# Feed-forward weights fetched from inside the plan and turned by the vector engine; variance of the last row pair by accumulated sums

## The chip, the cores and the metric

The kernel runs on one NeuronCore of a Trainium2 chip. The metric is the time of one execution on the device in microseconds (us), the median of several runs. A core has five engines that work side by side, each with its own queue of instructions taken strictly in order: PE (matrix products; its weight loads are shown apart as PEld), DVE (vector work), ACT (activation functions), POOL (general vector work) and SP, which here only issues DMA transfers. An instruction that waits holds up all that stands behind it on its engine.

## The reference

One transformer block on `x` of 4096 rows by 256 columns, all in float32: attention in which a row sees itself and the 127 rows before it, then a feed-forward part that mixes each row with the one before, a layer norm after each.

```python
q = (x @ Wq + bq)            # 16 heads of 16, 4 groups; k and v: 4 heads of 16
scores = q k^T / 4, masked to  i-128 < j <= i
x = layernorm(x + softmax(scores) v @ Wo + bo)
x_prev = x shifted down by one row
r = sigmoid((mu_r*x + (1-mu_r)*x_prev) @ W_r.T)
k = (mu_k*x + (1-mu_k)*x_prev) @ W_k.T
out = layernorm(x + r * (square(relu(k)) @ W_v.T))
```

`layernorm` subtracts the row's mean and divides by the root of its variance plus 1e-5. The three feed-forward weights are needed turned (columns on partitions), as `x` is for its products.

## The kernel before

The 4096 rows are cut into 8 chunks of 512 (index `c`) and 16 pairs of two 128-row blocks (index `p`, blocks `b`). The work of a chunk or pair is written as small operations, `op(kind, ...)`, each for one engine, with what it reads and writes, the ring buffers and PSUM banks that it takes, and a rank. `Plan.run` (L267) then fixes, at build time, the order of every engine's queue: the table `KINDS` (L34) gives each kind its engine, an assumed length and a rank; on PE the order is written out by hand in `ORDER` (L112), step by step; on the other engines, SP's queue included, the operation that can start first goes first, and among those within `WAIT` of it the one of lowest rank. Nothing is reordered on the chip.

A PE "step" below is one operation of `ORDER`. The kinds, with the line of their matmuls:

- `q` (L778, two per chunk) and `kv` (L730): projections from the turned `x` (`xT`); ACT copies them out of PSUM (`q copy` L789, `kv copy` L739). `vT` (L753) turns the v part; DVE copies it (L758).
- `q move` (L800): four DMAs on SP that copy half of the chunk's `q` to other partitions. The next kind needs all four.
- `maxima`, `maxima 2` (L842/L833 for masks, L855 for scores): row maxima of the scores of a pair, three steps for a pair, each on four of the eight PSUM banks; DVE reduces them (L865, two instructions a step, each frees two banks), turns the result (`nm turn`, L875), and four DMAs put it beside `q` (`nm put`, L879).
- `weights a` (two per pair) and `weights b` (L942 with masks L914/L928): scores again, now transposed, with the maxima taken off; ACT takes exponentials (L979, L1013). They need `nm put`.
- `values` (L1040, L1053), `wo` (L1180): the attention's output and projection; DVE turns and scales between them; then the norm (`plan_norm` L1107: statistics on DVE, scale on POOL, apply on ACT L1136).
- `fk` (L1296), `fr` and `fv` (L1323): the feed-forward products; between them ACT takes relu (L1306) and tanh (L1337), POOL the square (L1310) and the sum (L1355), DVE the gate (L1350).

Loads at the start stand in SP's queue in the order of the program text (L467 to L527): `x` of pairs 0 and 1, `Wk`, `Wv`, `Wq`, `x` of pairs 2 and 3, `W_k`, `W_r`, `W_v`, `Wo` (four DMAs), `bo`, `mu_r`, `mu_k`; after them come the planned ones. To the plan these are `given`, with an assumed time of landing, and `begin ...` stands for what each engine has to do before its first planned operation.

`x` is turned in one of two ways. For chunks 0 and 1 (pairs 0 to 3) PE transposes it against an identity, in four matmuls a pair (L619, and steps `xT`, L698), and ACT (or DVE) copies it out of PSUM. From chunk 2 on (`p > 3`, L683) a pair is loaded in four DMAs whose pieces are 256-byte runs (`turned_rows`, L452), so placed that one DVE instruction, which transposes 32 by 32 squares, finishes it (`turn_squares`, L458). The feed-forward weights are turned on PE (steps `w`, L666: four matmuls each) and copied out by ACT with a factor (L674; 0.5 for `W_v`).

The last pair (p = 15) has an own ending, `plan_last` (L1376), for each of its two blocks: PE product (L1383), gate (DVE L1395), sum (DVE L1399), statistics (DVE L1402, L1403), epsilon (DVE L1404), root (POOL L1409), apply (DVE L1414), store (L1419; the first from SP's queue, the second from ACT's).

Of the kernel before, what the change touches and what calls it, by code (L numbers as in the profile page):

```python
# [34 lines left out]
    "given": (SP, 0.0, -553.88),  # L35
    "begin pe": (PE, 1.7, 0),
    "begin act": (ACT, 6.5, -483.57),
    "begin dve": (DVE, 8.5, -417.58),
    "begin pool": (POOL, 5.3, -536.56),
    "begin sp": (SP, 8.0, -360.66),  # L40
    "w": (PE, 0.43, 0),
    "w copy": (ACT, 0.62, 0.22),
    "x load": (SP, 0.5, -0.16),
    "x turn": (DVE, 0.7, 28.13),
    "xT": (PE, 0.43, 0),
    "xT copy": (ACT, 0.6, -59.9),
    "kv": (PE, 1.72, 0),
    "kv copy": (ACT, 0.69, -12.4),
    "vT": (PE, 0.43, 0),
    "vT copy": (DVE, 0.4, -22.77),  # L50
    "ones": (SP, 0.6, -32.64),
    "q": (PE, 1.72, 0),
    "q copy": (ACT, 0.69, 43.86),
    "q move": (SP, 2, -8.69),
    "maxima": (PE, 0.88, 0),
    "maxima 2": (PE, 0.6, 0),
    "reduce": (DVE, 1.14, 17.06),
    "reduce 2": (DVE, 0.81, 10.47),
    "nm turn": (DVE, 0.21, -30.81),
    "nm put": (SP, 2.3, -10.21),  # L60
    "weights a": (PE, 0.95, 0),
    "exp a": (ACT, 1.02, 13.73),
    "weights b": (PE, 1.07, 0),
    "exp b": (ACT, 1.02, -18.72),
    "values": (PE, 2.7, 0),
    "oN": (DVE, 1.25, -54.27),
    "rs": (DVE, 0.35, 29.15),
    "at": (DVE, 0.9, 2.41),
    "attT": (DVE, 0.44, 30.81),
    "xres": (SP, 0.5, 55.18),  # L70
    "bo": (POOL, 1.3, -22.9),
    "wo": (PE, 1.72, 0),
    "y": (DVE, 0.69, 34.29),
    "x1T first": (POOL, 0.25, 45),
    "x1 out": (SP, 0.45, -21.17),
    "x1 in": (SP, 0.5, -30.3),
    "x1 turn": (DVE, 0.7, 32.58),
    "x1T": (PE, 0.43, 0),
    "x1T copy": (ACT, 0.6, -17.18),
    "xd": (POOL, 1.3, -31.81),  # L80
    "xm": (DVE, 0.45, 57.86),
    "fk": (PE, 1.72, 0),
    "relu": (ACT, 0.6, 20.57),
    "square": (POOL, 1.07, 41.45),
    "fr": (PE, 1.72, 0),
    "gate": (ACT, 0.6, 36.74),
    "fv last": (PE, 0.86, 0),
    "y2 last": (DVE, 0.42, -24.81),
    "stats last": (DVE, 1.1, 59.97),
    "scale last": (POOL, 0.8, -21.85),  # L90
    "apply last": (DVE, 0.46, -51.24),
    "fv": (PE, 1.72, 0),
    "y2": (DVE, 0.69, -26.87),
    "y2 add": (POOL, 1.3, 33.09),
    "y2 add late": (DVE, 0.69, 28.33),
    "store": (SP, 0.45, 32.89),
    "stats y": (DVE, 0.6, 21.13),
    "scale y": (POOL, 1.5, 51.83),
    "apply y": (ACT, 0.6, 31.11),
    "stats y2": (DVE, 0.6, 46.62),  # L100
    "scale y2": (POOL, 1.5, 26.69),
    "apply y2": (ACT, 0.6, 80.48),
# [4 lines left out]
    "x load": 0.45, "x1 in": 0.45, "q move": 1.6, "xres": 1.3, "x1 out": 1.3, "store": 1.3,  # L107
# [9 lines left out]
        5, 11, 19, 23, 37, 98, 105, 134,  # L117
    ],
    "q": [
        1, 2, 6, 13, 16, 26, 46, 51, 60, 76, 81, 92, 119, 124, 130, 138,  # L120
    ],
    "vT": [
        7, 36, 22, 66, 45, 115, 150, 173,
    ],
    "w": [
        29, 30, 10,
    ],
    "maxima": [
        9, 12, 17, 15, 32, 25, 35, 28, 48, 39, 62, 57, 73, 59, 75, 84,
        89, 100, 104, 91, 121, 118, 125, 110, 131, 145, 153, 137, 167, 156, 176, 171,  # L130
    ],
    "maxima 2": [
        8, 14, 24, 20, 47, 61, 56, 88, 99, 103, 117, 107, 144, 136, 152, 170,
    ],
    "weights a": [
        18, 27, 31, 38, 41, 44, 50, 52, 65, 68, 70, 77, 79, 86, 93, 95,
        112, 114, 123, 127, 133, 140, 147, 149, 158, 165, 174, 179, 185, 188, 192, 194,
    ],
    "weights b": [
        21, 34, 42, 53, 64, 71, 80, 96, 108, 128, 141, 159, 163, 180, 183, 189,  # L140
    ],
    "values": [
        33, 43, 49, 63, 72, 85, 90, 109, 122, 132, 146, 164, 175, 184, 193, 199,
    ],
    "wo": [
        40, 54, 69, 78, 83, 101, 111, 116, 142, 148, 160, 172, 182, 190, 198, 204,
    ],
    "fk": [
        55, 74, 87, 102, 120, 143, 151, 157, 162, 168, 186, 197, 201, 207, 209, 212,
    ],  # L150
    "fr": [
        58, 82, 97, 106, 126, 135, 155, 161, 169, 181, 191, 195, 203, 206, 211, 214,
    ],
    "fv": [
        67, 94, 113, 129, 139, 154, 166, 177, 178, 187, 196, 200, 205, 210, 213,
    ],
    "xT": [
        3, 4,
    ],
    "x1T": [  # L160
        202, 208,
    ],
    "fv last": [
        215, 216,
# [47 lines left out]
class Plan:  # L212
# [8 lines left out]
    WAIT = 0.35  # L221
# [145 lines left out]
def postln_block(  # L367
# [112 lines left out]
    def load_w(dst, w):  # L480
        nc.sync.dma_start(out=dst, in_=w.rearrange("(c p) n -> p c n", p=P))
        return dst

# [10 lines left out]
    for p in range(2, 4):  # L494
        load_x(p)
    ffn_l = {"r": wl_r, "k": wl_k, "v": wl_v}
    for k, w in (("k", W_k), ("r", W_r), ("v", W_v)):
        load_w(ffn_l[k], w)

    wo = const.tile([P, 2, D], F32, tag="wo", name="wo")  # L500
    for g in range(NG):
        nc.sync.dma_start(
            out=wo[32 * g : 32 * (g + 1), :, :],
            in_=Wo[64 * g : 64 * (g + 1), :].rearrange("(rp x) n -> x rp n", x=32),
        )
    bo_b = const.tile([P, D], F32, tag="bo_b", name="bo_b")
    nc.sync.dma_start(out=bo_b, in_=bo.partition_broadcast(P))


# [4 lines left out]
    muT = const.tile([P, 2, C2], F32, tag="muT", name="muT")  # L514
    with nc.allow_non_contiguous_dma(reason="small vectors, once"):
        for i, bias in enumerate((bk, bv)):
            nc.scalar.dma_start(
                out=rows[2:3, :].rearrange("o (g i d) -> o i g d", g=NG, i=2)[:, i],
                in_=bias.rearrange("(o g d) -> o g d", o=1, g=NG),
            )  # L520
        for o in range(2):
            nc.scalar.dma_start(
                out=rows[0:2, :].rearrange("r (g o d) -> o r g d", g=NG, o=2)[o],
                in_=bq.rearrange("(g o r d) -> o r g d", g=NG, o=2, d=DH)[o],
            )
        for w, mu in enumerate((mu_r, mu_k)):
            nc.sync.dma_start(out=muT[:, w, :], in_=mu.rearrange("(p c) -> p c", c=C2))  # L527
# [131 lines left out]
    def plan_weight(k, base, scale):  # L659
        key = ("wps", k)  # L660

        def turn():
            w4 = bank(key).rearrange("p (i o n) -> p i o n", i=C2, o=C2)
            for o in range(C2):
                for i in range(C2):
                    nc.tensor.transpose(  # L666
                        w4[:, i, o, :],
                        ffn_l[k][:, o, i * P : (i + 1) * P] if k == "v" else columns(ffn_l[k][:, o, :], i),
                        ident,
                    )  # L670

        def keep():
            ffnT[k] = const.tile([P, C2, D], F32, tag=f"w{k}T", name=f"w{k}T")
            nc.scalar.mul(ffnT[k], bank(key).rearrange("p (i n) -> p i n", i=C2), scale)  # L674

        op("w", base, turn, r=[("rest", k)], w=[("wps", k)], banks=[(key, 1)], mode="full")
        op("w copy", base, keep, r=[("wps", k)], w=[("w", k)], uses=[("wps", k)])
# [4 lines left out]
    def plan_load(p):  # L682
        if p > 3:  # L683
# [3 lines left out]
        else:  # L687
            op("given", p, lambda: None, w=[("x", p)], new=[(ring("x", 4), ("x", p))], late=(3.7, 4.5, 7.0, 7.8)[p])

    def plan_xT(p, base):  # L690
        c, h = divmod(p, 2)
        key = ("xT", c, h)

        def turn():
            ps = bank(key).rearrange("p (c b n) -> p c b n", c=C2, b=2)
            for ch in range(C2):
                for b in range(2):
                    nc.tensor.transpose(  # L698
# [815 lines left out]
```

## Time and profile before

| | |
|---|---|
| median of 3 runs | 346.14 us (344.85 to 346.62) |
| the profiled execution, its own time | 345.45 us |
| its span, first to last instruction | 343.7 us |
| PE busy | 331.5 us, 4729 matmuls |
| DVE busy | 268.9 us |
| ACT, POOL busy | 165.8, 124.8 us |
| mean granted PE clock | 0.986 |

The span is 1.75 us shorter than the time of the same execution; what lies around the span stays outside the profile. "Busy" of PE is modelled: matmuls overlap, so a stretch that shows PE as busy need not be free of waiting, and it is the starts of the matmuls that tell. The first 15 us carry the loads: the profile shows 242 GB/s there from 6.8 to 15.0 us against a mean of 72.

### The profile page before, as it was taken

How to read it: one execution, taken by the hardware profiler on the slowest of the kernel's cores; microseconds unless marked ns; L12 is line 12 of the kernel's file. 1: busy time of each engine (PE TensorE's matmuls, PEld its weight loads, DVE VectorE, ACT ScalarE, POOL GpSimd, SP SyncE). 2: the span in 40 equal slices, each digit the busy share in tenths (PEclk: the TensorE clock that was granted, in tenths of full speed). 3: DMA queues.
4: the chain of work that ended last, by engine and by line, in shares of the span. 5: the costliest groups of instructions: out<-in, count | busy, mean ns of one | idle time of the engine just before them, and what ended most of it. 6: DMA issues, size and time to landing. Idle time of an engine off the chain costs nothing.

```text
span 343.7 us, 11149 instructions
## 1 busy us (share of the span) xinstructions
PE 331.5 (96%) x4729; PEld 221.7 (64%) x4729; DVE 268.9 (78%) x494; ACT 165.8 (48%) x227; POOL 124.8 (36%) x220
## 2 busy tenths in 40 slices
PE   8899999999999999999999999999999999999991
PEld 6455566655765676567666656767767676678871
DVE  7067787778888859999789998698948897678675
ACT  2402554556337583272442645653762386834541
POOL 5200000111404334161326231427632765648773
PEclk9969999999999999999999999999999999999998
DMA  6842333121511243211123220322221224210002
GB/s 191 226 100 47 75 78 68 35 67 19 139 33 35 69 89 94 67 33 58 42 60 98 63 68 32 65 82 84 55 87 41 65 70 120 79 49 31 32 31 92
DMA packets 55062, 24.65 MB, mean 72 GB/s; under 512 B 40644, under 2 KB 54852, under 8 KB 55012
## 3 DMA queue, kind: packets, MB, share of 16 engines
q1 hardware_dynamic: 54832, 23.81, 26.3%
q8 instruction: 37, 0.61, 0.8%
q10 hardware_dynamic: 180, 0.13, 0.1%
q14 instruction: 13, 0.11, 0.1%
HBM read 13.64 MB, written 7.86 MB: 63 GB/s over the span
## 4 chain that ended last, share of the span: by engine, by line
PE 83%; DVE 7%; SPq 3%; POOL 2%; issue 1%; DMA 1%; ACT 1%; POOLq 0%; DVEq 0%
PE ps L1323 14%; PE ps L942 12%; PE ps L855 9%; PE ps L1040 8%; PE ps L1180 8%; PE ps L778 8%; PE ps L1296 7%; PE ps L1053 4%; PE ps L730 4%; PE ps L842 2%; PE ps L914 2%; DVE xm L1268 2%; SPq L800 2%; DVE nm L865 1%; PE ps L753 1%
## 5 line engine op out<-in xcount | busy, mean ns | idle before, releaser
L865 DVE TENSOR_REDUCE nm<-ps 128x6 f32<-128x960 f32 (+1 forms) x96 | 94.7, 1037 | 16.6 <-PE ps L855 15.0
L979 ACT ACTIVATE prA<-ps 128x1024 f32<-128x1024 f32 x64 | 63.2, 1024 | 56.7 <-PE ps L914 53.1
L942 PE MATMUL ps<-qT,kT 17*64 17x512 f32 (+1 forms) x1024 | 54.7, 499 | 0.0
L855 PE MATMUL ps<-kT,qT 16*128 16x160 f32 x1024 | 48.8, 309 | 2.4 <-DMA qT<-qT 2.3
L1124 POOL TENSOR_SCALAR ve_y<-mv_y 128x2 f32<-128x2 f32 x31 | 8.0, 257 | 96.2 <-DVE mv_y L1119 95.3
L855 PEld LDWEIGHTS ps<-kT,qT 16*128 16x128 f32 x1024 | 39.5, 188 | 4.6 <-DMA qT<-qT 3.3
L1268 DVE SCALAR_TENSOR_TENSOR xm<-xd,muT,x1T 128x256 f32<-128x256 f32 x64 | 36.1, 614 | 5.4 <-POOL xd L1260 4.3
L1013 ACT ACTIVATE prB<-ps 128x1024 f32<-128x1024 f32 x32 | 31.0, 1021 | 13.7 <-PE ps L914 12.7
L1260 POOL TENSOR_TENSOR xd<-x1T 128x512 f32<-128x512 f32 x16 | 16.6, 1040 | 43.8 <-DVE x1T L459 43.8
L1065 DVE STREAM_TRANSPOSE oN<-ps 128x1024 f32<-128x1024 f32 x16 | 20.0, 1248 | 15.5 <-PE ps L1053 15.4
L1180 PE MATMUL ps<-wo,attT 128*128 128x256 f32 x128 | 31.4, 388 | 0.3 <-ACT prA L979 0.2
L778 PE MATMUL ps<-xT,wq 128*128 128x512 f32 x64 | 31.2, 612 | 0.3 <-DVE wq L631 0.3
L1040 PE MATMUL ps<-prA,vA 128*32 128x256 f32 x512 | 30.9, 382 | 0.4 <-ACT prA L979 0.2
L1296 PE MATMUL ps<-xm,wkT 128*128 128x256 f32 x128 | 30.8, 383 | 0.0
L1323 PE MATMUL ps<-wrT,xm 128*128 128x256 f32 x128 | 30.8, 383 | 0.0
L1118 DVE BATCH_NORM_STATS2 st_y<-y 128x6 f32<-128x256 f32 x62 | 25.3, 408 | 6.2 <-POOL y L1355 5.6
L942 PEld LDWEIGHTS ps<-qT,kT 17*64 17x64 f32 x1024 | 19.6, 130 | 15.5 <-issue 7.7
L1355 POOL TENSOR_TENSOR y<-y,x 128x512 f32<-128x512 f32 x14 | 19.1, 1364 | 28.0 <-DVE y L1350 27.9
L1323 PE MATMUL ps<-wvT,kact 128*128 128x256 f32 x120 | 29.0, 385 | 0.2
L1171 POOL TENSOR_TENSOR xres<-xres,bo_b 128x512 f32<-128x512 f32 x16 | 20.3, 1271 | 23.1 <-DMA xres<-in_L_attn_x 20.1
L1323 PEld LDWEIGHTS ps<-wrT,xm 128*128 128x128 f32 x128 | 23.8, 190 | 5.2 <-issue 1.6
L1180 PEld LDWEIGHTS ps<-wo,attT 128*128 128x128 f32 x128 | 23.3, 190 | 4.9 <-ACT prA L979 1.1
(109 smaller groups left out, 478.1 us busy)
## 6 DMA issues: line engine op xcount, KB each, us to landing
xres<-in_L_attn_x SPq DMA_DIRECT2D x16, 256.0 KB
out<-res SPq DMA_DIRECT2D x15, 256.0 KB
x1d<-x SPq DMA_DIRECT2D x14, 256.0 KB
x1w<-x1d SPq DMA_DIRECT2D x56, 64.0 KB
x<-in_L_attn_x SPq DMA_DIRECT2D x48, 64.0 KB
qT<-qT SPq DMA_DIRECT2D x32, 64.0 KB
x<-in_L_attn_x SPq DMA_DIRECT2D x4, 256.0 KB
qT<-nmT SPq DMA_DIRECT2D x64, 4.0 KB
```

What stands on the lines that cost most here:

```text
L778: nc.tensor.matmul(ps, wq[:, ch, rp, :, :].rearrange("p g x -> p (g x)"), xT[c][:, ch, :], start=(ch == 0), stop=(ch == C2 - 1),)
L855: nc.tensor.matmul(sc[g // 2][:, g % 2, u * W : (u + 1) * W], qT[c][g0 : g0 + DH, (2 * p + j) % NB, s, :, :, :].rearrange("p o r i -> p (o ...
L865: nc.vector.tensor_reduce(nms[p % 2].rearrange("p g j s -> p g (j s)")[:, 2 * i : 2 * i + 2, lo:hi], two_banks(keys[i])[:, :, 0 : n * W].r ...
L942: nc.tensor.matmul(dst[g], kT[k, k0 : k0 + 64], qT[c][k, blk, r0 : r0 + nr, :, :, :].rearrange("p s o r i -> p (s o r i)"), start=start, s ...
L979: nc.scalar.activation(prA[b][:, 2 * i : 2 * i + 2, :], two_banks(keys[i]), AF.Exp)
L1013: nc.scalar.activation(prB[p][:, 2 * i : 2 * i + 2, :, :].rearrange("p g j n -> p g (j n)"), two_banks(keys[i]), AF.Exp,)
L1040: nc.tensor.matmul(av[32 * g : 32 * (g + 1), hf, j, :], vA[:, values_of(b, g)], prA[b][:, g, hf * H : (hf + 1) * H], start=(j == 0), stop= ...
L1118: nc.vector.bn_stats(s6, src()[:, b, :])
L1180: nc.tensor.matmul(ps[:, j, :], attT[2 * p + j][:, rp, :, :].rearrange("p s i -> p (s i)"), wo[:, rp, :], start=(rp == 0), stop=(rp == 1),)
L1268: nc.vector.scalar_tensor_tensor(dst[p][:, ch, :], st["d"][:, ch, :], muT[:, which, ch : ch + 1], x1T[p][:, ch, 0:H2], ALU.mult, ALU.add,)
L1296: nc.tensor.matmul(ps[:, o, :], ffnT["k"][:, ch, o * P : (o + 1) * P], xk[p][:, ch, :], start=(ch == 0), stop=(ch == C2 - 1),)
L1323: nc.tensor.matmul(ps[:, b, :], lhs[:, ch, b * P : (b + 1) * P], w[:, ch, :], start=(ch == 0), stop=(ch == C2 - 1),)
```

## The change

`W_k`, `W_r`, `W_v`, `Wo`, `bo`, `mu_r`, `mu_k` leave the program text and become planned operations. The three feed-forward weights are loaded in four 256-byte-run pieces each and turned by one DVE instruction each; `W_v` is halved in place by ACT. The steps `w` and their copies are gone from PE and ACT. Because the turned layout differs, `fk` reads the columns of `W_k` with a stride of two. `x` of pairs 2 and 3 is loaded in pieces and turned by DVE, so the steps `xT` and their ACT copies are gone too.

In the last pair the sum also accumulates each row's total; DVE makes minus the mean of it; ACT squares the centred row with an accumulated sum of squares (writing into the result's buffer, later overwritten); POOL makes variance plus epsilon of it and then the root; the apply adds minus the mean. 

All ranks of `KINDS` and the whole of `ORDER` are new, and `WAIT` goes from 0.35 to 0.42. PE has 212 steps instead of 217. The first steps were, after those before the plan:

```
before  q q xT xT kv q vT maxima2(0) maxima(0) w kv maxima(0) q maxima2(1) maxima(1) q maxima(1)
        weights-a(0) kv maxima2(3) weights-b(0) vT kv ...
after   q q kv vT q maxima(0) maxima(0) q maxima2(0) maxima2(1) maxima(1) maxima(1) kv
        weights-a(0) weights-b(0) q vT maxima2(2) maxima(2) weights-a(1) kv maxima(2) weights-b(1) ...
```

(the number in brackets is the pair, for weights-a the block). The last steps are `fr14 fk15 fv14 fr15 fv-last fv-last` before (after `fk14 fv13`) and `fr14 fv13 fk14 fk15 fv14 fr15 fv-last fv-last` after. SP's queue of the changed program reads, after `Wq`: first piece of x2, of x3; `bo`; `mu_r`; `mu_k`; three pieces of x2, of x3; first pieces of x4, x5, x6; `q move` of chunk 0; `ones`; three pieces each of x4, x5, x6; one of x7; `Wo` (four); three of x7; `q move` of chunk 1; `nm put` of pair 0; two `xres`; three pieces of `W_k`; `nm put` of pair 1; pieces of x8 to x11, `W_k`, `W_r`; and so on.

```diff
-    for p in range(2, 4):
-        load_x(p)
-    for k, w in (("k", W_k), ("r", W_r), ("v", W_v)):
-        load_w(ffn_l[k], w)
...
-    def plan_weight(k, base, scale):
+    def plan_weight(k, base):
+        tile_, w = late_w[k]
+        pieces = tile_.rearrange("p c d -> p (c d)").rearrange("p (b j c) -> p b j c", j=Q, c=C2)
         def turn():
...
+            turn_squares(ffnT[k], pieces)
+        for a in range(4):
+            op("w load", base, lambda a=a: turned_rows(a, pieces, w), w=[("wl", k, a)])
+        key = ("w", k)
+        op("w turn", base, turn, r=[("wl", k, a) for a in range(4)], w=[key])
+        if k == "v":
+            op("w half", base, lambda: nc.scalar.mul(ffnT[k], ffnT[k], 0.5), r=[key], w=[key])
...
-        if p > 3:
+        if p > 1:
             for a in range(4):
                 op("x load", p, lambda a=a: load_x_turned(p, a), w=[("x", p, a)], ...
...
-                        ffnT["k"][:, ch, o * P : (o + 1) * P],
+                        ffnT["k"][:, ch, o:D:C2],
...
-            nc.vector.tensor_tensor(y, y, x1[p][:, b, :], ALU.add)
-            nc.vector.bn_stats(s6, y)
-            nc.vector.bn_aggr(st["mv"], s6)
-            nc.vector.tensor_scalar(st["mv"][:, 1:2], st["mv"][:, 1:2], EPS, None, ALU.add)
+            nc.vector.scalar_tensor_tensor(y, y, 1.0, x1[p][:, b, :], ALU.mult, ALU.add, accum_out=total)
+            nc.vector.tensor_scalar(st["nmean"], total, -1.0 / D, None, ALU.mult)
+        def squares():
+            nc.scalar.activation(
+                res[p][:, b, :], y2s[p][:, b, :], AF.Square, bias=st["nmean"], accum_out=st["ssq"]
+            )
         def scale():
+            nc.gpsimd.tensor_scalar(ve, st["ssq"], 1.0 / D, EPS, ALU.mult, ALU.add)
             nc.gpsimd.tensor_tensor(st["rstd"], ve, nhalf[:, 0:1], ALU.pow)
         def apply():
             nc.vector.tensor_scalar(
-                res[p][:, b, :], y2s[p][:, b, :], st["mv"][:, 0:1], st["rstd"], ALU.subtract, ALU.mult
+                res[p][:, b, :], y2s[p][:, b, :], st["nmean"], st["rstd"], ALU.add, ALU.mult
             )
...
-            for k, t in (("k", 9.5), ("r", 10.5), ("v", 11.3), ("wo", 12.0), ("bo", 12.5), ("mu", 13.5)):
-                op("given", 0, lambda: None, w=[("rest", k)], late=t)
+            op("rest wo", 0, load_wo, w=[("rest", "wo")])
+            op("rest bo", 0, load_bo, w=[("rest", "bo")])
+            op("rest mu", 0, load_mu, w=[("rest", "mu")])
```

## The prediction, made before any run of the changed kernel

> **What bounds the kernel now.** First the page: busy time, clock, chain.
>
> ```profile
> span 343.7 us, 11149 instructions
> PE 331.5 (96%) x4729; PEld 221.7 (64%) x4729; DVE 268.9 (78%) x494; ACT 165.8 (48%) x227; POOL 124.8 (36%) x220
> PEclk9969999999999999999999999999999999999998
> PE 83%; DVE 7%; SPq 3%; POOL 2%; issue 1%; DMA 1%; ACT 1%; POOLq 0%; DVEq 0%
> ```
>
> PE sets the time, and the chain runs on it for 83%. As busy PE is modelled, I read the starts of its matmuls in the trace and compared each step's start-to-start time with the shortest of its kind. From 45 us to 331 us all excesses together are about 0.5 us: PE is issued without a break. Time that is not PE work lies at two ends only: 7.6 us lost in the first 42 us, and 8.0 us from the start of the last PE step (335.69) to the end. So I went there next, PE's timeline from 14 to 28 us, then SP's:
>
> ```profile
> 15.28 0.23 PE L842 MATMUL ps<-maskM,identR 32*128 32x128 bf16 x4
> 17.36 0.53 PE L855 MATMUL ps<-kT,qT 16*128 16x160 f32 x2 [1.85 <-DMA qT<-qT]
> 18.15 1.17 PE L855 MATMUL ps<-kT,qT 16*128 16x160 f32 x4 [0.25 <-DMA qT<-qT]
> 19.53 0.67 PE L855 MATMUL ps<-kT,qT 16*128 16x160 f32 x9 [0.22 <-DMA qT<-qT]
> 22.14 1.11 PE L666 MATMUL ps<-ident,wl_kact 128*128 128x128 f32 x4
> 23.04 3.62 PE L730 MATMUL ps<-xT,wkv 128*128 128x512 f32 x4
> ```
>
> ```profile
> 13.17 1.45 SPq L453 DMA_DIRECT2D x<-in_L_attn_x  x3
> 14.72 2.70 SPq L800 DMA_DIRECT2D qT<-qT  x4
> 20.45 6.90 SPq L453 DMA_DIRECT2D x<-in_L_attn_x  x12
> 30.58 2.34 SPq L879 DMA_DIRECT2D qT<-nmT  x4
> 33.01 2.62 SPq L800 DMA_DIRECT2D qT<-qT  x4
> ```
>
> The first maxima wait, group by group, for the four q moves (4.1 us), which SP issues only at 14.72 though ACT has copied q by 11.26: loads stand ahead. And then the clock:
>
> ```profile
> 15.00:20.00 5.00, 2.58 (x26) 1.55 (x27) 1.44 (x3) 0.64 (x1) 2.48 (x2) 1.00 0.67 141
> 20.00:27.00 7.00, 7.00 (x54) 4.13 (x50) 4.40 (x5) 0.90 (x2) 0.00 (x0) 0.53 0.44 99
> ```
>
> (stretch, then busy us of PE, PEld, DVE, ACT, POOL, then granted clock.) After the half-idle stretch PE runs at half clock to 27 us; kv takes 3.6 us there for 1.72 elsewhere. That loses 3.3 us more. DVE's end:
>
> ```profile
> 336.34 0.41 DVE L1395 SCALAR_TENSOR_TENSOR y<-sig,ps 128x256 f32<-128x256 f32 x1
> 336.78 0.42 DVE L1399 TENSOR_TENSOR y<-y,x 128x256 f32<-128x256 f32 x1
> 337.24 0.43 DVE L1402 BATCH_NORM_STATS2 st_last<-y 128x6 f32<-128x256 f32 x1
> 337.99 0.41 DVE L1395 SCALAR_TENSOR_TENSOR y<-sig,ps 128x256 f32<-128x256 f32 x1
> 340.39 0.41 DVE L1414 TENSOR_SCALAR res<-y,mv_last,rstd_last 128x256 f32<-128x256 f32 x1 [0.23 <-POOL rstd_last L1409]
> ```
>
> A block takes 1.65 us on DVE, and the second one's apply ends 4.46 us after the first one's gate began.
>
> **Part 1, five transposing steps leave PE.** Starts 10.37, 10.83, 11.31 for xT, 49.06 and 49.65 for two of w: about 0.46 a step, 2.3 for five. All lie on the engine that bounds: **-2.3**. With them five ACT copies of 0.6 go (L674, L705) and one halving of 0.6 comes; ACT is busy 48% and none of these ends a wait of PE, so 0. DVE gains five turns at 0.69 (L459): the two of x at some 9.5 to 11.6 us, where DVE now idles 8.6 us; the three weights' between reductions at 44 to 57 us, where DVE is the fullest neighbour. With no slack there they would show as up to 2.1; I take 0.
>
> **Part 2, the new PE order.** An eight-matmul step costs 1.73 from start to start among its like, 1.83 with another tile shape on one side, 1.92 on both: 0.1 a change of shape. The orders have 137 and 142 of them: **+0.5** (0 to 1).
>
> **Part 3, the head, walked through.** q, q stand (6.83, 8.65). kv takes 10.37; its copy ends 2.6 later as now (11.31 to 13.92), at 13.0, so vT starts at 13.05, a wait of 0.95 that xT used to fill. Then q from 13.6 to 15.4; x of pair 2 and 3 is there: pieces issued from 3.94 on at 0.5 each, the last near 8.7, landed in 2 to 3 us, turned by 11.6. SP: 14 issues from 3.94 on end near 10.6, the last (x6) held for x2's turn, so q move goes at 11.3, when ACT is done, and not at 14.72; the four end at 14.0, and the last lands 2.07 later as now (17.42 to 19.49), at 16.05. The maxima wait 0.6 instead of 4.1.
> Next comes a new wait. The six maxima steps of pairs 0 and 1 now stand together with but one q between; each pair of steps fills all eight banks, so DVE sets the pace: 8 x 1.147 + 4 x 0.816 = 12.4 us of L865 from 17.2 on. The sixth step starts when four steps are reduced, 17.2 + 2.3 + 2.3 + 1.63 + 1.63 + 0.2 = 25.3, and kv ends near 28.1. Weights-a then needs nm put 0. On SP, after the q move (14.0): ones 0.65, 17 loads at 0.49 to 23.0, q move of chunk 1 (its copy is ready near 21.0) 2.6, nm put 2.3, landed 1.1 after its end as now (32.91 to 34.02): **29.1**, against 34.72 now. Taking off the q step (1.85) and the three transposing ones (1.4, in part 1) that stand before it now and not then, 2.4 are gained. The maxima after vT then wait for four exponentials of 1.02 and a q copy, 1.1 us; now 0.5 is lost at that place. With the smaller waits 0.8 to 0.9 goes back: **-1.5** for the head. Later SP entries have slack: nm put 1 waits behind three weight pieces (1.5 us), lands near 35 and is wanted near 41; nm put 2, behind some 20 pieces, lands near 48, wanted near 58. Without slack a late one costs its lateness in full.
> Bounds: weights-a at 28.1, when kv ends, and nothing given back, -3.4; half clock again after the paced stretch (the row above, priced below), +1.5.
>
> **Part 4, the end.** fv14 now follows fk15 and waits for the sum (L1355, 1.4) and square (1.04) of POOL a little less than now; the fv-last wait of 0.46 goes, as kact15 is made during fr15: **-0.45**. In DVE's chain the two statistics instructions and epsilon (0.43 + 0.18 + 0.15) become one of 128x1 (0.15). The sum with accumulation isn't in the trace: between 0.42 (L1399) and 0.9 (the dearest L1268), I take 0.55. So a block needs 1.2, not 1.65. But behind it stand now: square on ACT (L1136 of that size, 0.6, plus 0 to 0.2 for the accumulator, the shortest ACT row), POOL 0.25 (L1124), then the root 0.55. And ACT's queue holds the apply of pair 14 ahead of the first square; that waits for POOL's nmr, 1.9 after the gate, and ends at 2.5. Squares 2.5 to 3.1 and 3.1 to 3.7; POOL 0.25, 0.55, 0.25, 0.55 to 4.8; apply to 5.25, for 4.46 now: **+0.8**, bounds -0.4 (ACT free at once) to +1.6. It sits on the path in full; with hops +0.9.
>
> **Sum.** -2.3 + 0.5 - 1.5 - 0.45 + 0.9, and +0.4 for waits that a new order has somewhere in 280 us (0 to 2) = -2.45. The profiled execution took 345.45 (span 343.7 and 1.75 around it), so 343.0; the median is 0.7 above it, so **343.7**.
>
> **Two rules against the rows.** Half clock came here after waits of 1.85 and less within some 5 us. The Trainium skill, TensorE: Matmul & The Clock Gate, "Why this matters for your kernels", asks only that idle gaps stay under about 3 us. By the rule no stretch of the new head is slowed; by the row the paced one (PE busy some 4 of 7 us from 20 to 27) may be, +1.4.
> Loads in pieces: twelve of 64 KB went out in 6.90 us, one each 0.57, and x turned in time. The page DMA: Bandwidth & Descriptors, "Specifications", wants 512 bytes or more for line rate; these runs have 256. If by that the eight pieces took twice the row's time, x would be turned near 15.6 and the sum be 2.0 worse, 345.7.
>
> **Rivals.**
> *No change*: DVE's pacing halves the clock from 27 to 34 us; 4.9 us of PE work then lose 2.45, less the 1.1 wait that is slower to arise: +1.4; and the end costs 2.0, not 0.9. 343.7 + 1.4 + 1.1 = 346.2. For it: the 0.53 row. Against: work fills 13 to 20 us without a gap over 0.6.
> *Slower*: SP's queue. nm put 0 stands behind q move 1, which waits for a q copy, which waits for DVE to free a bank. There is 2.0 of slack (21.0 against 23.0). Beyond it each us goes into the start of weights-a, with the clock's 3.3 on top as now; it decides when that copy ends later than about 24. At 25: 343.7 + 2 + 3.3 = 349. For it: SP already waited 4.3 us in three q moves. Against: the step that frees the bank, the first reduction, hangs on nothing but the first q move, and 2.0 is nearly two reductions of slack.
> *More than forecast*: no pacing loss, end free: 346.14 - 2.3 - 3.4 - 0.4 + 0.5 = 340.5; in the forecast's low end.
>
> **Numbers.** Forecast 0.55, no change 0.25, slower 0.20. Likeliest own range 340.5 to 345.5; to leave out 2 in 10 the range goes to 347.8. 0.5% (1.7 us) is about what a measurement tells from none: below 344.4 faster, 0.54; 344.4 to 347.9 same, 0.26; slower 0.20.
>
> **What would show it.** Right: q moves issued by 11.5 us; first maxima complete by 18; weights-a starting at 28 to 30; clock 1.0 in 13 to 27 us; PE starts unbroken from 50 us; the last apply some 5.2 us after its pair's first gate. Wrong: weights-a after 32, clock 0.5 past 27, PE waits on DVE's banks between 45 and 100 us, or an end no longer than now.

## The result, and the profile after

| | before | after |
|---|---|---|
| median of 20 runs each | 345.59 us (343.61 to 347.49) | 347.11 us (345.49 to 349.79) |
| after / before | | 1.0053 (95%: 1.0029 to 1.0076) |
| the profiled execution, its own time | 345.45 us | 349.63 us |
| its span | 343.7 us | 347.9 us |

The change makes the kernel about half a per cent slower; forecast was 343.7 us, 0.7% faster than the 346.14 known then. The profiled execution after is one of the longer of its 20; a second one, of 346.91 us, is used beside it. First the page after: span, busy time, clock, chain.

```profile
span 347.9 us, 11145 instructions
PE 333.2 (96%) x4709; PEld 219.3 (63%) x4709; DVE 269.6 (77%) x497; ACT 163.6 (47%) x227; POOL 127.1 (37%) x222
PEclk9995799999999999999999999999999999999998
PE 79%; DVE 8%; DMA 4%; SPq 2%; issue 2%; POOL 2%; ACT 1%; POOLq 0%; DVEq 0%; ACTq 0%
```

PE issues 20 matmuls fewer and is busy 1.7 us longer: the clock dips for longer, and DMA now stands in the chain for 4% instead of 1%.

To see where the time went I took each PE step's start-to-start length from the trace before (by its kind and its neighbours' shapes, median behind 45 us), summed them along each order, and subtracted the sum from the step's real start. What the difference grows by is time lost at that place (for the head this includes work at half clock).

| us | before | after | after, second profile |
|---|---|---|---|
| PE steps, up to the last two products | 319.2 | 316.2 | 316.2 |
| before the first step and lost by some 43 us | 14.5 | 17.7 | 15.4 |
| lost from there to the last two products | 1.0 | 4.3 | 3.7 |
| from the first of these to the end | 9.0 | 9.7 | 9.7 |
| span | 343.7 | 347.9 | 345.1 |

The rows depend on the lengths taken as reference: with means for medians the first row falls by 2.1 us from before to after and the third grows by 2.5, while the changes in the second and fourth stay as they are here within 0.1. So PE's work fell by 2 to 3 us, more than the 1.8 forecast, and all of it and more was lost in three places. The head first, SP's queue:

```profile
11.37 2.70 SPq L767 DMA_DIRECT2D qT<-qT  x4
14.93 6.10 SPq L450 DMA_DIRECT2D x<-in_L_attn_x  x10
21.07 1.86 SPq L495 DMA_DIRECT2D wo<-in_L_attn_Wo  x4
22.97 1.41 SPq L450 DMA_DIRECT2D x<-in_L_attn_x  x3
24.49 2.59 SPq L767 DMA_DIRECT2D qT<-qT  x4
27.18 2.35 SPq L846 DMA_DIRECT2D qT<-nmT  x4
```

The first q move goes at 11.37 as forecast. The seventeen loads behind it take 9.5 us, not 8.35, and the put of pair 0 (L846), whose maxima DVE had turned at 23.07, goes out at 27.18. PE's timeline of the same place:

```profile
22.88 0.26 PE L809 MATMUL ps<-maskM,identR 32*128 32x192 bf16 x2 [0.47 <-DVE nm L832]
...
26.41 3.78 PE L697 MATMUL ps<-xT,wkv 128*128 128x512 f32 x4
30.77 2.02 PE L909 MATMUL ps<-qT,kT 17*64 17x512 f32 x16 [0.58 <-DMA qT<-nmT]
...
35.28 3.49 PE L745 MATMUL ps<-xT,wq 128*128 128x512 f32 x4
```

PE waits for DVE's banks between the maxima, then `kv` takes 3.78 us for 1.98 at full clock, weights-a starts at 30.77, and q at 35.28 is slow as well. The clock, in stretches of 3.41 us (stretch, its length, then busy us of PE, PEld, DVE, ACT, POOL, then granted clock, DMA share, GB/s):

```profile
17.87:21.28 3.41, 3.35 (x32) 1.58 (x28) 3.41 (x4) 0.69 (x1) 0.00 (x0) 1.00 0.38 85
21.28:24.69 3.41, 2.33 (x54) 1.81 (x56) 3.38 (x7) 0.00 (x0) 0.00 (x0) 1.00 0.59 137
24.69:28.11 3.42, 3.42 (x28) 2.23 (x27) 3.42 (x4) 0.00 (x0) 0.00 (x0) 0.50 0.52 97
28.11:31.52 3.41, 2.83 (x11) 0.70 (x17) 3.36 (x6) 0.69 (x1) 0.00 (x0) 0.50 0.31 75
31.52:34.93 3.41, 3.41 (x79) 2.62 (x64) 0.03 (x1) 1.02 (x1) 2.33 (x2) 0.50 0.62 165
34.93:38.35 3.42, 3.42 (x20) 1.41 (x5) 0.00 (x0) 2.86 (x3) 0.20 (x1) 0.50 0.26 59
```

The stretch in which DVE paces PE (2.33 busy of 3.41) is followed by four at half clock, 13.65 us. Next the middle, DVE's timeline:

```profile
52.67 0.71 DVE L456 STREAM_TRANSPOSE wrT<-wl_xr 128x512 f32<-128x512 f32 x1 [2.10 <-DMA wl_xr<-in_L_ffn_W_r]
53.30 2.18 DVE L832 TENSOR_REDUCE nm<-ps 128x6 f32<-128x960 f32 x2
...
63.18 0.71 DVE L456 STREAM_TRANSPOSE wvT<-wl_kact 128x512 f32<-128x512 f32 x1 [1.13 <-DMA wl_kact<-in_L_ffn_W_v]
```

Two turns of weights stand at the head of DVE's queue and wait for their last piece to land; reductions whose banks are full stand behind them, and PE loses 0.99 us at 54.6 and 0.78 at 63.7. Late in the middle, DVE and then PE:

```profile
293.35 3.53 DVE L1235 SCALAR_TENSOR_TENSOR xm<-xd,muT,x1T 128x256 f32<-128x256 f32 x5
...
297.17 1.45 DVE L1045 TENSOR_TENSOR at<-oN,rs 128x512 f32<-128x512 f32 x1
298.54 0.67 DVE L1317 SCALAR_TENSOR_TENSOR y<-sig,ps 128x512 f32<-128x512 f32 x1
```

```profile
297.84 0.73 PE L909 MATMUL ps<-qT,kT 17*64 17x256 f32 x6
299.27 0.89 PE L909 MATMUL ps<-qT,kT 17*64 17x256 f32 x21 [0.70 <-DVE y L1317]
```

Weights-b of pair 15 stops after six matmuls: its next bank still holds a product of pair 8, and the gate that empties it (L1317) stands behind five `xm` and a 1.45 us `at`. 1.4 us are lost. And the end, ACT:

```profile
341.74 0.60 ACT L1103 ACTIVATE res<-y,nmr_y,rstd_y 128x256 f32<-128x256 f32 x1 [3.00 <-POOL nmr_y L1097]
342.25 0.49 ACT L1375 ACTIVATE res<-y,nmean_last 128x256 f32<-128x256 f32 x1
342.65 0.19 ACT L1375 ACTIVATION_READ_ACCUMULATOR res<-y,nmean_last 128x1 f32 x1
```

The first square waits behind pair 14's apply and needs 0.6 with the reading of its accumulator. The last apply ends 5.30 us after the pair's first gate (339.80 to 345.10), for 4.46 before; forecast was 5.25. From the start of the last product to the end it is 8.75 us, for 8.0.

### The profile page after: what moved, and what is told of

Its sections match the earlier page's. It is cut to its first block, busy times and chain, and to the rows that moved or that the text cites. A ratio compares the mean times of both kernels' runs of the same rounds, so it can differ in the third digit from the quotient of the medians.

```text
span 347.9 us, 11145 instructions
## 1 busy us (share of the span) xinstructions
PE 333.2 (96%) x4709; PEld 219.3 (63%) x4709; DVE 269.6 (77%) x497; ACT 163.6 (47%) x227; POOL 127.1 (37%) x222
## 4 chain that ended last, share of the span: by engine, by line
PE 79%; DVE 8%; DMA 4%; SPq 2%; issue 2%; POOL 2%; ACT 1%; POOLq 0%; DVEq 0%; ACTq 0%
PE ps L1290 14%; PE ps L909 14%; PE ps L822 8%; PE ps L1147 8%; PE ps L745 8%; PE ps L1007 8%; PE ps L1263 7%; DVE nm L832 4%; PE ps L1020 4%; PE ps L697 3%; PE ps L809 2%; PE ps L881 2%; DVE xm L1235 2%; SPq L767 1%; DMA xres<-in_L_attn_x 1%
## 5 line engine op out<-in xcount | busy, mean ns | idle before, releaser
L909 PE MATMUL ps<-qT,kT 17*64 17x512 f32 (+1 forms) x1024 | 58.7, 514 | 1.7 <-DVE y L1317 0.7
L1138 POOL TENSOR_TENSOR xres<-xres,bo_b 128x512 f32<-128x512 f32 x16 | 21.7, 1356 | 77.4 <-DMA xres<-in_L_attn_x 34.5
L822 PE MATMUL ps<-kT,qT 16*128 16x160 f32 x1024 | 47.1, 308 | 0.1
L822 PEld LDWEIGHTS ps<-kT,qT 16*128 16x128 f32 x1024 | 37.9, 187 | 1.5 <-issue 1.1
L1235 DVE SCALAR_TENSOR_TENSOR xm<-xd,muT,x1T 128x256 f32<-128x256 f32 x64 | 34.7, 589 | 2.6 <-POOL xd L1227 2.5
L745 PE MATMUL ps<-xT,wq 128*128 128x512 f32 x64 | 32.8, 639 | 1.2 <-DVE wq L625 1.2
L909 PEld LDWEIGHTS ps<-qT,kT 17*64 17x64 f32 x1024 | 20.4, 134 | 20.1 <-issue 6.7
L1290 PE MATMUL ps<-wvT,kact 128*128 128x256 f32 x120 | 29.1, 385 | 0.1
L1322 POOL TENSOR_TENSOR y<-y,x 128x512 f32<-128x512 f32 x14 | 18.6, 1326 | 27.7 <-DVE y L1317 27.6
L1263 PEld LDWEIGHTS ps<-xm,wkT 128*128 128x128 f32 x128 | 24.6, 196 | 3.8 <-issue 0.8
```

Source lines behind the costliest of these rows:

```text
L745: nc.tensor.matmul(ps, wq[:, ch, rp, :, :].rearrange("p g x -> p (g x)"), xT[c][:, ch, :], start=(ch == 0), stop=(ch == C2 - 1),)
L822: nc.tensor.matmul(sc[g // 2][:, g % 2, u * W : (u + 1) * W], qT[c][g0 : g0 + DH, (2 * p + j) % NB, s, :, :, :].rearrange("p o r i -> p (o ...
L909: nc.tensor.matmul(dst[g], kT[k, k0 : k0 + 64], qT[c][k, blk, r0 : r0 + nr, :, :, :].rearrange("p s o r i -> p (s o r i)"), start=start, s ...
L1235: nc.vector.scalar_tensor_tensor(dst[p][:, ch, :], st["d"][:, ch, :], muT[:, which, ch : ch + 1], x1T[p][:, ch, 0:H2], ALU.mult, ALU.add,)
L1263: nc.tensor.matmul(ps[:, o, :], ffnT["k"][:, ch, o:D:C2], xk[p][:, ch, :], start=(ch == 0), stop=(ch == C2 - 1),)
L1290: nc.tensor.matmul(ps[:, b, :], lhs[:, ch, b * P : (b + 1) * P], w[:, ch, :], start=(ch == 0), stop=(ch == C2 - 1),)
```

## The experiments

Ratios are to the kernel before, run beside each. The runs of kernels with this head spread by 3 to 6 us, so effects of 1 us or less are read in the traces; each trace is of one execution.

**Old ending.**
```diff
-nc.vector.scalar_tensor_tensor(y, y, 1.0, x1[p][:, b, :], ALU.mult, ALU.add, accum_out=total)
...
+nc.vector.tensor_tensor(y, y, x1[p][:, b, :], ALU.add)
+nc.vector.bn_stats(s6, y)
+nc.vector.bn_aggr(st["mv"], s6)
```


> The changed kernel with the ending of the last row pair as it was before the change: sum, statistics, epsilon on DVE, root on POOL, apply with the mean subtracted. Ranks, PE order and loads stay those of the changed kernel. Theory (the tail pays: from the start of the last PE step to the end 8.75 us in the changed kernel, 8.0 in the kernel before): the tail goes back to about 8.0 and the time falls by 0.7 to 0.8 us, 346.4 for 347.1 median. Rival (the tail's length comes from the new order of the last steps, not from the accumulated sums): tail stays at 8.6 to 8.8, no change of time.

Measured: from the last step's start to the end 8.00 us; 347.09 us, 1.0032 (1.0008 to 1.0056). The trace bears the theory out; the time alone couldn't show it.

**PE's order of the kernel before.**
```diff
-    "kv": [ 3, 13, 21, 38, 29, 74, 106, 117 ], ...
+    (before's ORDER without the five transposing steps)
```


> The changed kernel with PE's order taken from the kernel before, less the five transposing steps that no longer exist; loads in pieces, DVE turns, ranks and last ending stay those of the changed kernel. Theory (the loss sits in the new head: six maxima steps in a row that DVE paces, half clock behind them, weights-a at 30.8): with the old order the maxima are spread again, the loss is less, and the time falls below both, 343 to 345. Rival A (the new order is needed because the weights now come late; the old one waits for them or for x): PE waits where fk or the first chunk's maxima stand, time 347 to 352. Rival B (head order makes no difference, the late weights' turns in DVE's queue are the loss): 346.5 to 347.5, with waits of weights-a for DVE at 54 to 64 us again.

Measured: 361.4 us, 1.0394 (1.0341 to 1.0446). No theory foresaw this: weights-a of pair 0 started at 34.18, and 18 us were lost between 60 and 310 us, up to 3.3 us at one place (184 us). An order of PE and the ranks of the other queues belong together; with one of them exchanged, the run says nothing on the parts.

**The weights' pieces taken as landing later.**
```diff
-op("w load", base, ..., w=[("wl", k, a)])
+op("w load", base, ..., w=[("wl", k, a)], late=5.0)
```


> The changed kernel, but the plan takes each piece of a feed-forward weight to land 5 us later than it did; so the instruction on DVE that turns a weight gets a place further back in DVE's queue, and nothing else but DVE's order of these turns and of neighbouring reductions moves. Theory (two of the turns stand in DVE's queue before their last piece has landed, 2.1 and 1.1 us, and hold up reductions; weights-a waits 1.0 at 54.6 us and 0.8 at 63.7): both waits go, the time falls by 1.0 to 1.75 us, to 345.4 to 346.1. Rival (the reductions are late for themselves, DVE is full there): the same waits of 0.5 to 1 us stay or move to the next step, the time stays within 0.4 us of 347.1.

The edit makes the plan count 5.0 us from the end of a load's issue to its landing, where it counted 1.3 (`LAND`): 3.7 later, not the 5 that the expectation says.

Measured: 346.08 us, 1.0015 (0.9983 to 1.0047), an interval that overlaps the changed kernel's; it is the trace that shows the effect. DVE's two turns wait for nothing now, and nor does PE between 40 and 89 us:

```profile
50.35 0.70 DVE L456 STREAM_TRANSPOSE wrT<-wl_xr 128x512 f32<-128x512 f32 x1
...
61.38 0.71 DVE L456 STREAM_TRANSPOSE wvT<-wl_kact 128x512 f32<-128x512 f32 x1
```

**The q move behind the put.**
```diff
-op("q move", base, move, r=[("qe", c, 0), ("qe", c, 1)], ...)
+op("q move", base, move, r=[("qe", c, 0), ("qe", c, 1)] + ([("qm", 0)] if c == 1 else []), ...)
```


> The changed kernel, but the four DMAs that move q of chunk 1 are put behind the four that put the maxima of pair 0 in SP's queue; elsewhere nothing but the neighbouring entries of that queue moves. Theory (weights-a waits for the put, which was issued at 27.2 to 29.5 us only because the q move stood ahead of it, though DVE had turned these maxima at 23.1): put issued from about 24.5, landed near 28, weights-a of pair 0 at 28 to 29.5 instead of 30.8; 1 to 2 us less at that place, of which q move 1 gives a part back at the maxima of pair 2; time 345.5 to 346.5. Rival (kv, which ends at 30.2 since it runs at half clock, sets the start): weights-a stays at 30.2 to 30.8 and the time within 0.4 us of 347.1, or above it by the later q move.

Measured: put issued at 24.80, yet weights-a at 31.09, when `kv` ended: at that place the rival holds (first SP, then PE).

```profile
24.80 2.32 SPq L846 DMA_DIRECT2D qT<-nmT  x4
```
```profile
27.38 3.78 PE L697 MATMUL ps<-xT,wkv 128*128 128x512 f32 x4
31.09 1.61 PE L909 MATMUL ps<-qT,kT 17*64 17x512 f32 x16
```

The time was 346.48 us, 1.0014 (0.9987 to 1.0041). W_r's turn also came later in DVE's queue (58.23, no wait), so a gain in the middle is mixed in.

**kv between the maxima.**
```diff
-q maxima2(0) maxima2(1) maxima(1) maxima(1) kv weights-a(0)
+q maxima2(0) kv maxima2(1) maxima(1) maxima(1) weights-a(0)
```


> The changed kernel with one PE step in another place: the projection kv of chunk 1 stands between the two maxima steps of pair 0 and pair 1 that used to follow one another, instead of behind all six maxima steps; a few loads move in SP's queue with it. Theory (PE half idle while DVE paces it brings the half clock): kv fills the pause of 0.4 to 0.6 us a step, the clock keeps 1.0 longer or the half stretch is one window of 6.8 us and never two; weights-a of pair 0 no longer waits for kv at 28 to 31 us but for the maxima, whose put is issued at 27.2 as before: start 30.5 to 30.8, and the steps behind it at full clock; time 345 to 346. Rival (the clock does not follow what PE does here, or kv holds up the maxima and DVE with them): last maxima and put later by up to 1.9, time 347 to 349.

Measured: 349.83 us, 1.0118 (1.0084 to 1.0152). `kv` is done by 22.9 at full clock, and PE stands for the put:

```profile
31.20 2.01 PE L877 MATMUL ps<-qT,kT 17*64 17x512 f32 x16 [4.74 <-DMA qT<-nmT]
```

The idle stretch (1.10 us busy of 3.41 from 24.97 on) brings half clock for 10.24 us. SP issued the put at 27.59, 0.4 later than in the changed kernel. So the put alone would have set the start of weights-a to about 31: `kv` only hid it.

**The fr product of pair 10 first.**
```diff
-weights-a(31) weights-b(15) wo(14) fr(10)
+weights-a(31) fr(10) weights-b(15) wo(14)
```


> The changed kernel with one PE step in another place near the end: the fr product of pair 10 stands ahead of weights-b of pair 15 and wo of pair 14 instead of behind them. Theory (weights-b waits 1.4 us at 297.8 for a bank that DVE's gate frees late, behind five xm instructions): the product fills the wait, weights-b finds its bank free; the wait of 1.3 to 1.5 is gone and the time falls by as much, to 345.7. Rival (DVE is late as a whole there, so the wait moves to the next step that needs DVE, wo or values of pair 15): the same 1 to 1.5 us reappear within 10 us, time within 0.4 of 347.1.

Measured: no wait at weights-b nor within 30 us behind it; the theory holds there. The time, 347.18 us with a spread of 344.0 to 349.6, 1.0016 (0.9983 to 1.0049), doesn't settle it by itself.

**More work for PE in the maxima.**
```diff
+if p == 1 or (p == 0 and unit == 2):
+    for _ in range(3):
+        nc.tensor.matmul(..., eye, maskM[g0 : g0 + 32, 0:n, :, :], start=True, stop=False, ...)
```


> The changed kernel with PE given more to do, and nothing else: in the maxima steps of pair 0 (the last) and pair 1 the matmuls that write the masks are issued four times instead of once, the last of them standing; the output is the same. That is 48 matmuls more, some 1 us a step, within the 1.6 to 2.3 us that DVE needs for a step. Theory (PE half idle in 18 to 25 us brings the half clock that follows): the clock stays 1.0 past 25 us or the half stretch is a single short window, and kv, weights-a, q and vT behind it take their full-clock times; 1.5 to 4 us less in 25 to 45 us, time 344 to 346 with the upper runs near 349 gone. Rival (the half clock has another cause: a fixed time after the start, or load of another kind): half clock as before for 6.8 or 13.7 us, and time equal or up to 0.5 to 1 us longer by the extra matmuls.

Measured: 350.2 us, 1.0136 (1.0101 to 1.0170). The clock stayed at 1.0 until 31.97 us, 7 us longer, and `kv` ran at full clock; then PE stood for the put, and half clock came behind that:

```profile
25.79 1.98 PE L697 MATMUL ps<-xT,wkv 128*128 128x512 f32 x4
31.99 2.01 PE L919 MATMUL ps<-qT,kT 17*64 17x512 f32 x16 [4.21 <-DMA qT<-nmT]
```

In this kernel the half clock moved with PE's pause, and SP's put held up the head though `kv` ran at full clock.

**All mendings**: the old ending, the late pieces, the q move, kv and fr as above, and `late=-1.0` for the last pair's relu, which puts POOL's square ahead of a norm.

> The changed kernel with all that the runs so far name mended at once: old ending of the last pair; the feed-forward weights' pieces taken as landing 5 us later, so that DVE turns them later; q move of chunk 1 behind the put of pair 0; kv of chunk 1 between the maxima steps of pair 0; the fr product of pair 10 ahead of weights-b of pair 15; and POOL's square of the last pair ahead of the norm of pair 13. Theory (each loss is its own and they add): tail 8.0 for 8.75, 1.7 less in the middle, 1.3 less at 298 us, 0.5 less at the last product, 1.5 to 3 less in the head: from 347.1 to 340.5 to 342.5, under the kernel before by 1 to 1.5%. Rival (the losses stand for one another: DVE or the clock takes back what one mending gives): 344 to 346, no better than before.

Measured: 343.03 us, 0.9925 (0.9903 to 0.9947), and runs within 342.67 to 344.20: faster than both. SP's put goes at 24.41, and weights-a starts 2.8 us earlier than after the change:

```profile
27.94 1.12 PE L876 MATMUL ps<-qT,kT 17*64 17x512 f32 x16 [1.17 <-DMA qT<-nmT]
```

By the account of the first table: 316.4 of steps, 15.2 in the head, 1.0 in the middle, 9.0 at the end. Against the kernel before only PE's steps differ by much. The theory's range, 340.5 to 342.5, was missed by 0.5 us. In the head, where it counted on 1.5 to 3 us, 15.2 were lost for 17.7 and 15.4 in the two profiles of the changed kernel and 14.5 in the kernel before, which has half clock for 6.83 us, as this one has.

**The two head edits alone**, kv between the maxima and the q move behind the put.

> The changed kernel with two of the edits together that were run alone before: kv of chunk 1 between the maxima steps of pair 0, and the q move of chunk 1 behind the put of pair 0 in SP's queue. Alone they gave 1.0118 and 1.0014 of the kernel before. Theory (two things end at about the same time ahead of weights-a of pair 0, the put on SP and kv at half clock on PE; taking away one leaves the other, and moving only kv makes PE idle longer before the put, so that the half clock lasts longer): together weights-a starts at 27.5 to 28.5 us for 30.8, time 0.99 to 1.0 of the kernel before, less than either alone. Rival (the edits add): 1.0118 and 1.0014 against 1.0053 give 1.008.

Measured: weights-a at 28.12 as the theory had it, but 351.23 us, 1.0166 (1.0135 to 1.0197), worse than either alone. SP's new order holds W_r's second half back to 56.00, and DVE stands for it (first SP, then DVE, then PE):

```profile
46.72 0.94 SPq L418 DMA_DIRECT2D wl_xr<-in_L_ffn_W_r  x2
...
56.00 0.94 SPq L418 DMA_DIRECT2D wl_xr<-in_L_ffn_W_r  x2
```
```profile
58.48 0.71 DVE L424 STREAM_TRANSPOSE wrT<-wl_xr 128x512 f32<-128x512 f32 x1 [2.29 <-DMA wl_xr<-in_L_ffn_W_r]
```
```profile
60.29 2.82 PE L1115 MATMUL ps<-wo,attT 128*128 128x256 f32 x8 [2.23 <-DVE nm L800]
```

5.4 us are lost from 41 to 70 us, and a second half-clock stretch follows the pause (6.83 us from 61.32 on). With the late pieces, in the kernel with all mendings, PE loses nothing there with the same head edits.

**Three variations of the mended kernel.** More mask matmuls; then the put ahead of Wo, the weights' pieces and the residual; then both.
```diff
-op("xres", base, load, w=[("xres", p)], ...)
+op("xres", base, load, r=[("qm", 0)], w=[("xres", p)], ...)
```
(and `r=[("qm", 0)]` likewise for `w load` and `rest wo`, planned after the maxima of pair 0)

> The kernel with all mendings (343.0 median, 0.9925), and its mask matmuls in the last maxima step of pair 0 and in those of pair 1 issued four times, as was tried on the changed kernel alone. There the clock stayed 1.0 to 32 us, but PE then stood 4.2 us for the put. Here the put comes 3 us earlier. Theory (a window of 3.4 us in which PE is idle for more than about 0.8 us brings half clock in the next): no or only a short half-clock stretch in 25 to 40 us; 1.5 to 3.5 us less, 339.5 to 341.5. Rival (PE is idle for the put at 26.8 to 27.9 in any case, and that alone sets the half clock; the extra matmuls delay the maxima): half clock of 6.8 us as before, 343 to 344.

> The kernel with all mendings (343.0 median, 0.9925), with Wo, the feed-forward weights' pieces and the residual's loads put behind the put of pair 0 in SP's queue; the order of DVE's turns of the weights moves with it. Theory (SP is late: the maxima of pair 0 are turned at 23.0, their put issued only at 24.4): put issued from 23.1, landed at 26.6, weights-a of pair 0 at 26.7 to 27.0 for 27.9, no PE pause ahead of it; 1 to 1.3 us less there, or 2 to 4 if the half clock then shortens as well: 339.5 to 342. Rival (the loads, now later, are waited for: Wo and the residual by wo of pair 0 near 50 us, W_k by fk of pair 0 near 96): new waits after 45 us, time 343 or more.

> Both: the put of pair 0 ahead of Wo, the weights' pieces and the residual, and the mask matmuls four times in the last maxima step of pair 0 and those of pair 1. Theory (with PE busy through the maxima and no pause for the put, no window is idle enough): clock 1.0 from 12 to 40 us without a half stretch or with one of 3.4 us, 338.5 to 340.5. Rival (something else than PE's pauses sets the half clock): a half stretch of 6.8 us stays somewhere in 20 to 40 us and the time is that of the put alone, 341 to 342, or more by the extra matmuls.

Measured: 343.84 us, 0.9950 (0.9926 to 0.9975), with half clock for 6.83 us as before; 342.87, 0.9925 (0.9902 to 0.9949), with weights-a at 26.63 but half clock for 10.24 us; and 344.03, 0.9945 (0.9914 to 0.9976). The profile of the last has no half-clock stretch at all before the end, at 341.40 us:

```profile
PEclk9999999999999999999999999999999999999998
```

There the head lost some 12 us by the account of the first table, 2 to 3 less than in the kernel before and in the mended one. Its other runs reach 345.56, and the clock goes with it: the four shortest, 341.40 to 342.17, have a mean clock of 0.995 or more, and six of the seven others, 342.63 to 345.56, one of 0.986 to 0.988 (the seventh, 344.63, has 0.994). As far as a mean clock tells, the extra work kept the half clock away in some executions only. With the mask matmuls alone the rival holds (343 to 344); with the put alone weights-a came as early as the theory had it, but the time did not (339.5 to 342); with both the theory holds for the clock of the one profile, not for the time (338.5 to 340.5). None of the three is surely faster than the mended kernel.

**Middle and end mended, head untouched.**

> The changed kernel with the head as it is, and the mendings behind it alone: the feed-forward weights' pieces taken as landing 5 us later, so that DVE turns them later; the fr product of pair 10 ahead of weights-b of pair 15; old ending of the last pair; POOL's square of the last pair ahead of the norm of pair 13. Theory A (the head costs nothing against the kernel before but for a second half-clock stretch in some executions; the loss lies behind it): 341.5 to 343.5, as fast as the kernel with all mendings or faster, with some runs 3 us above. Theory B (the head loses by itself, SP's put and kv): 344.5 to 346, 2 us or more above the kernel with all mendings (343.0).

Measured: 345.05 us (341.96 to 346.26), 0.9966 (0.9938 to 0.9994). The median is in theory B's range, while the shortest runs are in A's. Its profile (346.26 us) lost 17.7 in the head with half clock for 13.65 us, and 1.3 behind it. The shortest run, 341.96, is as short as any of the mended kernel (342.67), the longest 2 us over its longest (344.20). Five of the six longest runs have a mean clock of 0.977 to 0.979 (345.88 has 0.986), the five shortest, up to 344.30, one of 0.986 or 0.987: here too the clock goes with the longer times, though it doesn't tell the shorter ones apart.

**The square alone, on the kernel before.**

> The kernel before with one edit: POOL's square of the last pair stands ahead of the norm of pair 13, by telling the plan that its relu is ready 1 us sooner; nothing else moves but the place of one norm instruction on ACT. It tells how much of the best kernel's gain was to be had without the change. In that kernel this edit and the old ending gave a tail of 7.34 for 8.0 and took away the wait of the last product. Theory (POOL's order sets both): wait of 0.46 gone and tail 7.3 to 7.4, time lower by 0.9 to 1.1, ratio 0.997. Rival (in the old order of the last steps POOL is free in time anyway): time unchanged within 0.3.

Measured: 345.34 us, 0.9993 (0.9973 to 1.0014). The first of the last two products starts 1.72 us after the product ahead of it, for 2.08 before, but the end, counted from that first one, stays 9.0 us, as in the mended kernel. The time fits the rival (unchanged within 0.3 us), not the theory's ratio of 0.997. The "7.34" of the expectation was my misreading: it counted from the second product, which had itself come to start 0.7 later. So this edit alone gives next to nothing without the change; whether another order or other ranks would gain in the kernel before wasn't tried.

**The changed kernel again.**

> The changed kernel as it is, once more. Its first profile had half clock for 13.65 us in the head, two windows of 6.83, and a time of 349.6; its median is 347.1. Theory (the length of the half-clock stretch is what spreads its runs): a profile of 346 to 347 us shows one window of 6.83 or less, and the offset behind the head is about 3 us smaller (14 to 15 for 17.5), with the same waits of weights-a at 54 and 64 us, 1.4 at 298 us and 8.75 at the end. Rival (the runs are spread by the waits in the middle): the same half-clock stretch, and other waits behind 45 us.

Measured: 346.25 us, 1.0033 (1.0006 to 1.0060); the profile of 346.91 us is the second one of the first table. Half clock for 3.41 and 6.83 us, 15.4 in the head, 1.4 at 298 us and the same end; the waits near 54 and 63 us were smaller, 0.45 and 0.72. The theory had one half-clock stretch of 6.83 us or less; there were two with 10.24 in all, for 13.65 in the first profile. So the shorter half clock and smaller waits in the middle both took part.

## Why the prediction was wrong

The sum said -2.45; median against median, +1.5 was measured. The 347.11 us lie outside the likeliest range (340.5 to 345.5) and inside the wide one (to 347.8). By its steps:

- **Parts 1 and 2 (-2.3 and +0.5, together -1.8): right in sign, somewhat small.** PE's steps shrank by 2 to 3 us. The two parts weren't measured apart.
- **Part 1's zero for DVE's turns: failed.** "With no slack there they would show as up to 2.1; I take 0." They cost 1.8 in the first profile and 1.2 in the second, and not because DVE was full: a turn in a strict queue waits for its DMA with everything behind it. The edit that moves only their places removes the waits, and the head pair, which makes the pieces later, raises the loss to 5.4.
- **Part 3's head (-1.5): failed.** The walk to the first maxima was right (`x` of pairs 2 and 3 was turned by 11.84 us, for 11.6 forecast and 15.6 if its pieces had taken twice the row's time), the one from there to weights-a was not. Weights-a, forecast at 29.1, started at 30.6 to 32.0 in six profiles with this head, and the loss by 43 us moved by -0.2 to +3.2, by +1.6 in the mean. The term that was mis-sized is SP's seventeen loads: they took 9.5 us for the 8.35 I summed, which made the put 1.5 us late. I took 0.49 a load, though the row that I showed, twelve loads in 6.90 us, gives 0.57 each and 9.8 in all. The other is the clock: `kv` at half clock ended as late, so removing either cause alone left the other. The row I weighed against the skill's rule (PE busy 4 of 7 us) was the one to follow: 2.33 busy of 3.41 us were followed by half clock for 13.65 us, which I had left to the rival's 0.25. The Trainium skill, TensorE: Matmul & The Clock Gate, "Why this matters for your kernels", asks for no idle gap over about 3 us; the waits in that stretch were of 0.2 to 0.5 us each, so by the rule the clock would have stayed up, and the measurement decides.
- **The middle (+0.4): too small.** Beside the turns, 1.4 went at 298 us and 0.6 at 112 us.
- **Part 4: +0.9 right** (+0.75; the apply at 5.30 for 5.25), **-0.45 failed**: the first of the last two products still started 2.08 us after the one ahead of it, as before the change, since POOL's order put a norm ahead of the square.

Of the rivals, "no change" (half clock past 27 us) had the mechanism that cost most in the longer runs. "Slower" named the place, the put behind q move 1, but wanted the q copy to be late; it was SP itself.

## What to carry to other kernels

A load that moves from the program's start into a planned queue brings a consumer with it: give the plan a landing time that is too long rather than too short, since an early place in a strict queue blocks everything behind it (here 1.2 to 1.8 us of PE, and none with 5.0 us). When two causes end at the same time, mend both before judging either. And change a hand-made order only together with the ranks that were made for it.

## What the hardware showed

- Half clock came in stretches of 3.41, 6.83, 10.24 and 13.65 us, all multiples of 3.41, the first of each head at 18.8 to 32.0 us. In the 3.41 us ahead of each of the 22 stretches in these traces (leaving out the one behind each trace's last products) PE was busy for 0 to 3.2 us, mostly below 2.8. The converse doesn't hold: in the kernel before, 1.99 busy of 3.41 (13.53 to 16.94) was followed by full clock, so the busy time of one such stretch alone doesn't decide it. Executions of one kernel differ: of the changed kernel's 20 runs the seven with a mean clock under 0.98 have a median of 348.87 us, the thirteen others 346.65, though two of these took 348.70 and 349.49. The Trainium skill, TensorE: Matmul & The Clock Gate, "Part 1: The HAM clock gate", describes a window of 3413 ns that is free-running; the lengths bear out the 3413 ns. That the place of this window sets how long the half clock lasts is shown by no run here.
- POOL's instruction held up DVE's. The sum at L1322 took 1.57 us on DVE when POOL's square had begun 0.02 earlier (first DVE, then POOL, of the changed kernel; the kernel before has the same pair):

```profile
337.11 1.57 DVE L1322 TENSOR_TENSOR y<-y,x 128x512 f32<-128x512 f32 x1
```
```profile
337.09 1.04 POOL L1277 TENSOR_TENSOR kact<-kr 128x512 f32<-128x512 f32 x1
```

  The same sum took 0.69 where the square had ended before it, in the kernel before with the one edit to POOL's order:

```profile
333.43 0.69 DVE L1355 TENSOR_TENSOR y<-y,x 128x512 f32<-128x512 f32 x1
```

  The excess, 0.88, is about the rest of the square, 1.02. The Trainium skill, SBUF — State Buffer, "SBUF: two separate sides", says that whichever of such a pair starts first holds the port that they share for its whole instruction, and that the other is blocked; the rows agree within 0.14 us, and the `at` at 297.17, 1.45 us for 0.69 beside a square from 297.03 to 298.07, does too.
- Accumulating cost little here: reading the accumulator took 0.08 us on DVE and 0.19 on ACT. What cost was the longer chain.
